# A graph attention kernel: sets of thirteen nodes in place of twelve, other first members, and the second maps and the row turn in other PSUM places

## The chip, the core and the metric

One core of one Trainium2 chip runs the whole kernel as one program. The metric is device microseconds of that core from launch to end. The kernel before took 861.07 to 866.28 us in three runs, median 863.03.

## What is computed

Eight graphs of 2048 nodes share one 0/1 matrix of neighbours. Every node has 64 features. A first attention layer with four heads and a second with one head are followed by a residual sum and a layer norm.

```python
def gat_layer(h, mask, b):                       # h: [..., N, D]
    scores = einsum('...nd,...md->...nm', h, h)
    scores = where(mask, scores, -1e16)
    return einsum('...nm,...md->...nd', softmax(scores), h) + b

B, N, C, H, D = 8, 2048, 64, 4, 64
mask = graph + eye(N) > 0
h     = einsum('bnc,hdc->bhnd', x, Wh)
out_h = gat_layer(h, mask, bh)
cat   = transpose(out_h, (0, 2, 1, 3)).reshape(B, N, H * D)
z     = leaky_relu(cat, 0.2)
h2    = einsum('bnk,dk->bnd', z, Wo)
out2  = leaky_relu(gat_layer(h2, mask, bo), 0.2)
mu, var = mean(out2, -1), mean((out2 - mu) ** 2, -1)
g     = (out2 - mu) * rsqrt(var + 1e-5) * gamma + beta
return layernorm(x + g)
```

The matrix is sparse and uneven: node n has a weight that falls with the root of n, so that the first nodes have very many neighbours and late ones few.

## The kernel before, in words

**Sets and pairs.** The first HUB = 56 nodes (the hub) attend densely to all 2048. The other 1992 make 166 sets (NS) of SET = 12 nodes each. Set s holds the nodes 56 + s + 166 k for k from 0 to 11: one of each of twelve blocks of 166 consecutive nodes. A set has one list of the nodes that any of its members has as a neighbour, at most 127 long; attention of the set is worked out against the gathered rows of that list, and a mask takes out what is not a neighbour of the member at hand. A list that doesn't fit sets a flag, and a general kernel then does all again. Two sets are a pair (NG = 83 pairs); the first layer takes one step for each pair. Four sets are a unit (NU = 42), eight sets a block (NV) in the second layer.

**First stretch.** The rows of x are loaded (`load_x` L458, the first four blocks on ACT's queue), extended and written to a table in DRAM; the hub's rows of the matrix are loaded (`hubraw` L474), and the hub's attention runs over the 16 blocks of 128 nodes (scores L621 on PE, mask L625 on DVE, exp L628 on ACT). Beside it the sets' rows of the matrix come in pieces of 10 sets by 1024 columns (`load_adj`: DMA L706, cut to 0 and 1 by POOL L711, own columns set to 1 by two selects L718). PE folds a piece to one key per column (the node's number with one bit for each member), and DVE picks the largest keys, eight at a time (`MAX` L767 and `MATCH_REPLACE` L769): these are the list. The lists are made in rounds of FIRST = 60 sets; the first round falls into the first stretch, the later ones into the loop below.

**The loop over pairs** (i from -3 to NG + 2). All engines run their own programs in the order written here; the code is scheduled by hand, and only semaphores stand between the engines. Step i holds work on several pairs:

1. scores of pair i+1 (PE L858), weighed by DVE (`weigh` L863) and exponentiated by ACT (`lift` L870)
2. head maps of pair i-1 (`project`, PE L551), leaky part on ACT (`leaky` L538), finished on DVE (L543)
3. values of pair i (`values`, PE L883), divided by their sums on DVE (`invert`: two reciprocals L890, one product L891 into `osb`)
4. a gather of the rows of pair i+5 (POOL L829), and copies on POOL
5. second maps of pair i-2 (`second_maps`, PE L917), copied out by DVE (`keep_own` L922)
6. row turn of pair i-3, a transpose (`second_rows`, PE L927); DVE adds a bias (`keep_rows` L931) and SP writes rows to a second table in DRAM
7. columns for pair i+4 (PE L843), copied out by ACT (`keep_columns` L849)
8. four transposes of gathered rows of pair i+3 (`turn`, PE L532), turned values of pair i (`turn_values`, PE L900, read by ACT in `keep_values` L907), and four more transposes

A step's picks for later lists follow on DVE behind point 6.

PSUM holds three tiles of two banks in this loop, each with one buffer: S for scores (`sp`), C for `cat`, O for `op`, and two more banks for the transposed rows. What shares a tile with what is said by columns. In `cat`, 0 to 192 of both banks hold the head maps (2 GM wide, GM = 96), 192 to 384 the columns, 384 to 480 of the first bank the second maps and 384 to 512 of the second the row turn:

```python
            ph, pr = cat[:, 0, 384:384 + GM], cat[:GM, 1, 384:512]
```

In `op`, each bank is cut in two parts of 256 columns; the first 132 of a part hold the values with their sums, and the 112 behind them the turned values:

```python
        return op.rearrange("a j (k c) -> a (j k) c", k=2)[:, :, 2 * (D + 2):2 * (D + 2) + 112]
```

In the middle of the loop, two steps for each block of eight sets, SP loads the blocks' own rows of x into `xbs` (`load_own` L961), POOL adds beta, and SP writes them to a third table (L965).

**Second layer and end.** The rows of the second table are gathered again, one list after the other (POOL L829, `rows`), with scores, exp and values on units of four sets. Every block of eight sets gets its norm (`norm`, mostly DVE), its rows of x from the third table, and is stored in eight DMAs (L1400), on SP's queue, the last block on three queues in turn.

Of the kernel before, what the change touches and what calls it, by code (L numbers as in the profile page):

```python
# [36 lines left out]
OP = mybir.AluOpType  # L37
# [7 lines left out]
HUB = 56  # L45
SET = 12
# [313 lines left out]
def fast_kernel(ctx: ExitStack, tc: tile.TileContext, x, adj, Wh, bh, Wo, bo, gamma, beta, out, flag):  # L360
# [13 lines left out]
    NS = (N - HUB) // SET  # L374
    NG = NS // 2
# [3 lines left out]
    FIRST = 60  # L379
    NR = (NS + FIRST - 1) // FIRST  # L380
    S10 = 10
    HALFN = N // 2
    NHB = (NS + S10 - 1) // S10
    assert NS * SET == N - HUB and NG * 2 == NS and HUB % 4 == 0 and NS % 2 == 0
# [31 lines left out]
    share = [const.tile([P, n], F32, name=f"share{k}") for k, n in enumerate([HALFN, HALFN, HALFN, 512, 512, 2 * 456])]  # L416
# [24 lines left out]
    es = [early.tile([P, 912], F32, name=f"e{k}") for k in range(2)]  # L441
# [31 lines left out]
    for k in range(2):  # L473
        nc.sync.dma_start(out=hubraw[k], in_=adj[0:HUB, k * NCH:(k + 1) * NCH])  # L474
# [18 lines left out]
    def make_powers():  # L493
        nc.gpsimd.memset(powers, 0.0)
        d = powers[:, :126].rearrange("p (g c) -> p g c", g=3)[:, :, :10]
        for k in range(SET):
            nc.gpsimd.affine_select(out=d, in_=d, pattern=[[0, 3], [-1, 10]], base=-10 * k, channel_multiplier=1,
                                    compare_op=OP.not_equal, fill=float(N << k))
# [6 lines left out]
        for row in (0, 32):  # L505
            nc.gpsimd.memset(adds[row:row + 1], 1.0)
        for h in range(2):
            for row, src in ((0, count[0:1, :n].unsqueeze(2).to_broadcast([1, n, SEG // 2])),
                             (32, count[32:33, h * 4:h * 4 + 4].unsqueeze(1).to_broadcast([1, n, SEG // 2]))):
                nc.vector.tensor_copy(number[row:row + 1, h, :].rearrange("p (q j) -> p q j", q=n), src)  # L510

# [71 lines left out]
    def hub_by_sets(c):  # L583
        k = slice(c * SET // 4, (c + 1) * SET // 4)
        nc.scalar.copy(hubs.rearrange("n (s k) -> n s k", k=SET)[:, :, k],
                       hubm[:, HUB:].rearrange("n (k s) -> n s k", s=NS)[:, :, k])

    def hub_mask_sets():
        pm = two("pms")
        cols = hubs  # L590
        for b in range(NHB):
            s0, ns = hub_sets(b)
            nc.tensor.matmul(pm[:ns * SET, b // 9, b % 9 * HUB:(b % 9 + 1) * HUB], cols[:, s0 * SET:(s0 + ns) * SET], identb[:HUB, :HUB],
                             start=True, stop=True)
        for b0, n in ((0, 9), (9, NHB - 10), (NHB - 1, 1)):
            np_ = hub_sets(b0)[1] * SET
            nc.vector.tensor_scalar(maskt[:np_, b0:b0 + n, :].rearrange("p b n -> p (b n)"),
                                    pm[:np_, b0 // 9, b0 % 9 * HUB:(b0 % 9 + n) * HUB], 0.0, 255.0, OP.is_equal, OP.mult)
# [54 lines left out]
    def hub_later(t, new):  # L653
# [19 lines left out]
        def to_table():  # L673
# [11 lines left out]
            dst = table2[:HUB, :].rearrange("n (q c) -> q n c", q=Q)  # L685
            for k in range(2):
                nc.sync.dma_start(out=dst[2 * t + k], in_=r[k * HUB:(k + 1) * HUB])
# [10 lines left out]
    byset = adj[HUB:, :].rearrange("(k s) m -> k s m", s=NS)  # L698

    def load_adj(r, t, m):  # L700
# [5 lines left out]
        nc.sync.dma_start(out=raw[:np_], in_=byset[:, s0:s0 + ns, m * NCH:(m + 1) * NCH])  # L706
# [6 lines left out]
        if m == 1:  # L713

            c0 = (HUB + s0) // 2
            for h in range(2):
                d = a[:np_, h, c0:c0 + NS // 2 * SET].rearrange("p (k c) -> p k c", k=SET)[:, :, :ns // 2]
                nc.gpsimd.affine_select(out=d, in_=d, pattern=[[-ns, SET], [-2, ns // 2]], base=-h,  # L718
                                        channel_multiplier=1, compare_op=OP.not_equal, fill=1.0)

    def powers_of(ns, g):
        return powers[:ns * SET, g * 32:(g + 1) * 32] if ns == S10 else powers6[:ns * SET, g, :]

    last = NS % S10
    powers6 = early.tile([120, 3, 32], BF16, name="powers6")
    if last:
        nc.gpsimd.memset(powers6, 0.0)

    def make_powers6():
        g = in_round[NR - 1] // S10 % 3  # L730
        d = powers6[:last * SET, g, 10 * g:10 * g + last]
        for k in range(SET):
# [815 lines left out]
```

## Time and profile before

| what | us |
|---|---|
| median of three runs | 863.03 |
| lowest and highest run | 861.07, 866.28 |
| the profiled execution's own time | 860.43 |
| its span (first to last instruction in the trace) | 858.6 |
| mean granted PE clock over the span | 0.97 |
| gathers of the first layer (POOL L829, 166) | 175.6 busy |
| gathers of the second layer (POOL L829, 166) | 173.7 busy |
| chain that ended last: PE, DVE, DMA | 61%, 17%, 9% of the span |

The trace is of one execution, whose own time is 1.8 us longer than its span. Busy times of an engine add up its instructions; PE is its matmuls, PEld the weight loads beside them. The chain is followed back from the last instruction to whatever released each one.

### The profile page before, as it was taken

The page shows a single profiled execution, that of the slowest core. Times are in us where ns is not written, and L with a number is a line of the kernel's source. Part 1 is how long each engine was busy: PE and PEld are TensorE (multiplying, and loading weights), DVE is VectorE, ACT ScalarE, POOL GpSimd, SP SyncE. Part 2 cuts the span into 40 slices and gives each one's busy share as a digit, 9 for nine tenths or more (in the row PEclk, how much of TensorE's full clock was granted, in tenths as well). Part 3 has the DMA queues.
Part 4 walks back from the last instruction along what each step waited for, and adds up shares of the span by engine and source line. Part 5 has one row for each costly group of instructions (what it writes and reads, how often), then busy time and mean ns, then how long its engine had stood idle before and what let it go on. Part 6 is the DMA issues. An engine that isn't in the chain of part 4 may idle for free.

```text
span 858.6 us, 42821 instructions
## 1 busy us (share of the span) xinstructions
PE 760.2 (89%) x18461; PEld 651.4 (76%) x18461; DVE 601.5 (70%) x1368; ACT 537.9 (63%) x1175; POOL 485.3 (57%) x619
## 2 busy tenths in 40 slices
PE   4798788899999999999999999998999899998940
PEld 3575567788888898988998988887887778876730
DVE  4347974688887788886556665564248999997895
ACT  2354545566666666666666666663558889887741
POOL 5444563564454456655665666504777777777700
PEclk9899989999999999999999999999999999999975
DMA  6999652443333344444444444335975666665621
GB/s 124 214 243 268 192 171 53 111 118 89 92 88 89 83 118 134 129 120 129 128 130 120 123 123 117 90 108 146 310 202 170 181 189 193 191 180 166 185 55 34
DMA packets 81791, 122.53 MB, mean 143 GB/s; under 512 B 35568, under 2 KB 51852, under 8 KB 81594
## 3 DMA queue, kind: packets, MB, share of 16 engines
q0 software_dynamic: 26784, 65.84, 28.7%
q1 hardware_dynamic: 50374, 52.71, 21.5%
q8 instruction: 148, 2.42, 1.2%
q10 hardware_dynamic: 4436, 1.15, 0.7%
q14 instruction: 49, 0.40, 0.2%
HBM read 123.91 MB, written 18.48 MB: 166 GB/s over the span
## 4 chain that ended last, share of the span: by engine, by line
PE 61%; DVE 17%; DMA 9%; issue 5%; SPq 3%; ACT 3%; POOL 2%; DVEq 0%; POOLq 0%; ACTq 0%
PE o L883 10%; PE s L858 9%; PE bank L532 8%; PE cat L843 6%; DMA rows<-table,index 5%; PE cat L551 4%; PE o L900 3%; PE cat L917 3%; PE t L532 3%; SPq L1400 3%; PE oh L639 3%; PE cat L927 2%; PE sh L621 2%; DMA out_dram<-y_s 2%; PE o L1317 2%
## 5 line engine op out<-in xcount | busy, mean ns | idle before, releaser
L829 POOL DMA_INDIRECT g<-table,index x166 | 175.6, 1058 | 173.6 <-PE o L883 144.8
L829 POOL DMA_INDIRECT rows<-table,index x166 | 173.7, 1046 | 55.1 <-issue 23.2
L863 DVE TENSOR_TENSOR e<-s,mask 128x768 f32<-128x768 f32 x83 | 79.3, 955 | 73.5 <-PE s L858 70.3
L538 ACT ACTIVATE z<-cat,bhp 128x192 f32<-128x192 f32 x166 | 60.7, 416 | 79.4 <-PE cat L551 79.3
L532 PE MATMUL t<-ident,rows 128*128 128x128 f32 x664 | 93.0, 279 | 11.2 <-DMA rows<-table,index 5.2
L883 PE MATMUL o<-g,e 128*64 128x65 f32 x2656 | 97.9, 225 | 3.9 <-issue 3.8
L532 PE MATMUL bank<-ident,g 128*128 128x128 f32 x664 | 99.5, 273 | 1.4 <-DVE e L1059 1.2
L883 PEld LDWEIGHTS o<-g,e 128*64 128x64 f32 x2656 | 85.4, 138 | 14.6 <-issue 4.8
L858 PEld LDWEIGHTS s<-y,xTg 64*64 64x64 f32 x5312 | 85.2, 135 | 13.8 <-issue 13.8
L858 PE MATMUL s<-y,xTg 64*64 64x48 f32 x5312 | 95.5, 221 | 0.0
L1436 ACT COPY xts<-t 128x512 f32<-128x512 f32 x166 | 88.7, 583 | 8.6 <-PE t L532 7.7
L532 PEld LDWEIGHTS t<-ident,rows 128*128 128x128 f32 x664 | 72.9, 141 | 24.0 <-issue 12.2
L1182 ACT COPY xTg<-bank 128x512 f32<-128x512 f32 x166 | 89.0, 596 | 2.5 <-PE bank L532 2.5
L532 PEld LDWEIGHTS bank<-ident,g 128*128 128x128 f32 x664 | 79.0, 141 | 4.1 <-issue 1.3
L849 ACT COPY y<-cat 128x384 f32<-128x384 f32 (+1 forms) x82 | 41.6, 508 | 64.1 <-PE o L900 34.5
L870 ACT ACTIVATE e<-e,shifts 128x768 f32<-128x768 f32 x83 | 80.1, 965 | 2.0 <-DVE e L863 2.0
L711 POOL TENSOR_SCALAR a<-raw 120x1024 bf16<-120x1024 int32 (+1 forms) x34 | 38.5, 1134 | 65.5 <-DMA raw<-in_adj_dram 50.6
L628 ACT ACTIVATE e<-e,shifts 128x896 f32<-128x896 f32 x32 | 33.4, 1043 | 58.1 <-DVE e L625 47.8
L890 DVE RECIPROCAL rall<-o 64x8 f32<-64x8 f32 x166 | 33.9, 205 | 47.8 <-PE o L883 46.5
L843 PE MATMUL cat<-xo,gram 128*128 128x192 f32 (+1 forms) x328 | 66.6, 326 | 0.0
L891 DVE TENSOR_TENSOR osb<-o,rall 128x512 f32<-128x512 f32 x83 | 57.4, 692 | 2.9
L625 DVE TENSOR_TENSOR e<-sh,maskh 128x896 f32<-128x896 f32 x32 | 34.8, 1087 | 31.6 <-PE sh L621 26.6
(195 smaller groups left out, 1529.8 us busy)
## 6 DMA issues: line engine op xcount, KB each, us to landing
raw<-in_adj_dram SPq DMA_DIRECT2D x32, 480.0 KB
table<-xb SPq DMA_DIRECT2D x22, 256.0 KB
xr_s<-table SPq DMA_DIRECT2D x21, 256.0 KB
table<-x SPq DMA_DIRECT2D x16, 260.0 KB
table<-rowt SPq DMA_DIRECT2D x164, 24.4 KB
xb<-in_x_dram SPq DMA_DIRECT2D x164, 24.0 KB
out_dram<-y_s SPq DMA_DIRECT2D x162, 24.0 KB
x<-in_x_dram SPq DMA_DIRECT2D x24, 128.0 KB
```

The costliest lines, as they stand in the source:

```text
L532: nc.tensor.transpose(tp[:, q * P:(q + 1) * P], rows[:, q, 1:1 + P], ident)
L538: nc.scalar.activation(z[:, hp], cat[:, :, hp * n:(hp + 1) * n], AF.Identity, bias=bhp[:, hp:hp + 1], scale=1.0)
L829: nc.gpsimd.indirect_dma_start(out=t.rearrange("n q c -> n (q c)"), out_offset=None, in_=table, in_offset=bass.IndirectOffsetOnAxis(ap=ind ...
L843: nc.tensor.matmul(cat[:, k, 2 * GM:2 * GM + n], gram[:, g % 2 * 2 + k, :], held["x", g // 2][:, :n], start=True, stop=True)
L849: nc.scalar.copy(held["y", g // 2][:, :n, g % 2 * 2:g % 2 * 2 + 2], cat[:, :, 2 * GM:2 * GM + n].rearrange("p a n -> p n a"))
L858: nc.tensor.matmul(sp[half(r), p, (q * 2 + j) * M:(q * 2 + j + 1) * M], xt[half(p), j, q, half(r)], y[half(p), (j * Q + q) * M:(j * Q + q ...
L863: nc.vector.tensor_tensor(e[:, :16 * M].rearrange("p (a q n) -> p a q n", a=2, q=Q), sp[:, :, :8 * M].rearrange("p a (q n) -> p a q n", q= ...
L870: nc.scalar.activation(e[:, :16 * M], e[:, :16 * M], AF.Exp, bias=shifts[:, 0:1], scale=1.0)
L883: nc.tensor.matmul(op[half(p), j, o0:o0 + K1], e[:, c0:c0 + 64], rw[j][:, q, sums(p)], start=True, stop=True)
L891: nc.vector.tensor_tensor(osb, v[:, :, :, 1:K1], r.unsqueeze(3).to_broadcast([P, 4, 2, D]), OP.mult)
L1182: nc.scalar.copy(t[:, k, :], bank[k])
L1436: nc.scalar.copy(xts[s // 2 % 4][:, s % 2, :], tp)
```

## The change

What it does:

- HUB becomes 60 columns of which BASE = 59 are nodes; SET becomes 13. 2048 - 59 = 1989 nodes make 153 sets. That is 77 pairs; the last pair is sets 151 and 152, so it does set 151 again (`set0`). Units are 39, the last with one set. A member's width M goes from 48 to 52, GM from 96 to 104.
- The first member of set s is no longer the node at s of the first block but the one 72 further round it (`firsts`). Nodes are thus told by positions in the order of sets, and `spans` says which runs of nodes stand at which positions. Loads of x, of the hub's rows of the matrix and stores follow these runs, in more and smaller DMAs. A piece of the matrix is 9 sets and two DMAs (108 and 9 rows); its own columns are set by six selects in place of two. A third row in `number` brings a position's key back to the node's number.
- FIRST becomes 54, 6 times 9.
- The second maps (`ph`) leave `cat` and are written into `op`, columns 132 to 236 of its first bank. The turned values go to columns 0 to 116 of each part of `op`, where the values were. The row turn (`pr`) is two transposes of 64 rows, into columns 416 to 480 of both banks of `cat`.
- The own rows of x have one buffer for two, and go in 12 DMAs for eight sets where there were 8; the stores likewise.

The diff, cut to what the prediction speaks of:

```diff
-HUB = 56
-SET = 12
+HUB = 60
+BASE = 59
+SET = 13
+ROT = 72
...
-    NS = (N - HUB) // SET
-    NG = NS // 2
+    NS = (N - BASE) // SET
+    NG = (NS + 1) // 2
...
-    FIRST = 60
+    S10 = 9
+    FIRST = 6 * S10
...
+    def firsts(s0, n):
+
+        while n > 0:
+            a = (s0 + ROT) % NS
+            w = min(n, NS - a)
+            yield s0, BASE + a, w
+            s0, n = s0 + w, n - w
+
+    def spans(p0, n):
+
+        for a, b, shift in ((0, BASE, 0), (BASE, BASE + NS - ROT, ROT), (BASE + NS - ROT, BASE + NS, ROT - NS), (BASE + NS, N, 0)):
+            lo, hi = max(a, p0), min(b, p0 + n)
+            if lo < hi:
+                yield lo, lo + shift, hi - lo
+
+    def set0(g):
+        return min(2 * g, NS - 2)
+
+    def quad(m):
+        s0 = min(4 * m, NS - 2)
+        return s0, min(4, NS - s0)
...
         for p in range(2):
-            (nc.scalar if i < 4 else nc.sync).dma_start(out=t[:, :, 1 + p * D:1 + (p + 1) * D],
-                                in_=x[p::2, i * P:(i + 1) * P, :].rearrange("q n c -> n q c"))
+            for at, node, n in spans(i * P, P):
+                (nc.scalar if i < 4 else nc.sync).dma_start(out=t[at - i * P:at - i * P + n, :, 1 + p * D:1 + (p + 1) * D],
+                                    in_=x[p::2, node:node + n, :].rearrange("q n c -> n q c"))
...
-        nc.sync.dma_start(out=raw[:np_], in_=byset[:, s0:s0 + ns, m * NCH:(m + 1) * NCH])
+        nc.sync.dma_start(out=raw[ns:np_], in_=byset[1:, s0:s0 + ns, m * NCH:(m + 1) * NCH])
+        (_, node, n), = firsts(s0, ns)
+        nc.sync.dma_start(out=raw[:ns], in_=adj[node:node + n, m * NCH:(m + 1) * NCH])
...
     OQ = 256
+    RC = 64 + M
...
     def turned(op):
-        return op.rearrange("a j (k c) -> a (j k) c", k=2)[:, :, 2 * (D + 2):2 * (D + 2) + 112]
+        return op.rearrange("a j (k c) -> a (j k) c", k=2)[:, :, :RC]
...
     def second_rows(g, pr):
-        nc.tensor.transpose(pr, held.pop(("own", g)), ident)
+        t = held.pop(("own", g))
+        for p in range(2):
+            nc.tensor.transpose(pr[:, p, :], t[half(p)], ident[half(p), half(p)])
...
-    xbs = [early.tile([P, 8, D], F32, name=f"xb{k}") for k in range(2)]
+    xbs = [early.tile([P, 8, D], F32, name="xb")]
...
         cat = one(f"cat{i}", "C") if i <= NG else None
-        if i < NG:
-            ph, pr = cat[:, 0, 384:384 + GM], cat[:GM, 1, 384:512]
-        else:
+        if i > NG:
             cat = one(f"cat{i}", "S" if i == NG + 1 else "C")
-            ph, pr = cat[:, 0, :GM], cat[:GM, 1, :P]
+        pr = cat[:GM, :, 4 * GM:4 * GM + D]
...
             op = one(f"o{i}", "O")
+            ph = op[:, 0, 2 * (D + 2):2 * (D + 2) + GM]
             values(i, op)
             invert(i, op)
+        if i >= NG:
+            ph = cat[:, 0, 2 * GM:3 * GM]
...
         if 0 <= i - 2 < NG:
             second_maps(i - 2, ph)
```

**PE, step 40 of the loop, from the last values to the turned values.** In the rows that follow the left name is what an instruction writes, the right ones what it reads (`o` is the tile `op`, `cat` the tile `cat`, `z` the leaky head maps, `own` the second maps copied out, `bank` the transposed rows, `osb` the divided values); then rows by columns, and the engines that it waits for. Before:

```order
L883 MATMUL o40_6614<-g1_81_6050,e0_110 64x65 x2
L917 MATMUL cat40_6598<-z38_6492,woT_93 64x2x4x12 [waits Activation_49]
L917 MATMUL cat40_6598<-z38_6492,woT_93 64x2x4x12 x3
L927 MATMUL cat40_6598<-ident_78,own37_6538 96x128
L843 MATMUL cat40_6598<-xo22_6406,gram_92 128x192 [waits Pool_49]
L843 MATMUL cat40_6598<-xo22_6406,gram_92 128x192
L532 MATMUL bank0_1747<-ident_78,g1_86_6398 128x128 [waits DMASW3_49,Activation_49]
L532 MATMUL bank0_1747<-ident_78,g1_86_6398 128x128 x3
L900 MATMUL o40_6614<-ident_78,osb40_6631 128x112 [waits DVE_49]
L900 MATMUL o40_6614<-ident_78,osb40_6631 128x112 x3
```

The same place of the change:

```order
L921 MATMUL o40_6886<-g1_81_6309,e0_110 64x65 x2
L955 MATMUL o40_6886<-z38_6763,woT_93 64x2x4x13 [waits DVE_49]
L955 MATMUL o40_6886<-z38_6763,woT_93 64x2x4x13 x3
L967 MATMUL cat40_6870<-ident_78,own37_6810 104x64 [waits Activation_49]
L967 MATMUL cat40_6870<-ident_78,own37_6810 104x64
L880 MATMUL cat40_6870<-xo22_6672,gram_92 128x208 [waits Pool_49]
L880 MATMUL cat40_6870<-xo22_6672,gram_92 128x208
L560 MATMUL bank0_1919<-ident_78,g1_86_6664 128x128 [waits DMASW3_49,Activation_49]
L560 MATMUL bank0_1919<-ident_78,g1_86_6664 128x128 x3
L938 MATMUL o40_6886<-ident_78,osb40_6903 128x116 [waits DVE_49]
L938 MATMUL o40_6886<-ident_78,osb40_6903 128x116 x3
```

The order of the kinds of work is the same. The second maps (L917, now L955) write `o40` where they wrote `cat40`, and wait for DVE where they waited for ACT; the row turn (L927, now L967) is two matmuls for one and now carries the wait on ACT; the turned values (L900, now L938) wait for DVE as before.

**DVE, the same step, from the reciprocals to the row copy.** `rall` holds the reciprocals of the sums, `own38` is the copy of the second maps, `rowt1` the rows for the second table. Before:

```order
L890 RECIPROCAL rall_100<-o40_6614 64x8 [waits PE_49]
L890 RECIPROCAL rall_100<-o40_6614 64x8
L891 TENSOR_TENSOR osb40_6631<-o40_6614,rall_100 128x512 [waits DVE_49]
L543 SCALAR_TENSOR_TENSOR z39_6607<-z39_6607 128x384 [waits Activation_49]
L922 COPY own38_6661<-cat40_6598 128x96 [waits PE_49,Pool_49]
L931 TENSOR_TENSOR rowt1_113<-cat40_6598,bob_95 96x128 [waits DMAHW1_49,DMAHW0_49]
```

And of the change:

```order
L928 RECIPROCAL rall_100<-o40_6886 64x8 [waits PE_49]
L928 RECIPROCAL rall_100<-o40_6886 64x8
L929 TENSOR_TENSOR osb40_6903<-o40_6886,rall_100 128x512 [waits DVE_49]
L571 SCALAR_TENSOR_TENSOR z39_6879<-z39_6879 128x416 [waits Activation_49]
L960 COPY own38_6938<-o40_6886 128x104 [waits PE_49,Pool_49]
L971 TENSOR_TENSOR rowt1_113<-cat40_6870,bob_95 104x128 [waits DMAHW4_49,DMAHW3_49,PE_49]
```

The order stands. The copy of the second maps (L960) reads `o40`, which the reciprocals and the product read too; the row copy (L971) carries a wait on PE of its own.

**ACT, at the start of the program.** `x0` and `x1` are the first two blocks of x, `whT` the transposed weights, copied out of PSUM. Before:

```order
L458 DMA x0_120<-in_x_dram 128x4x64 x2
L458 DMA x1_122<-in_x_dram 128x4x64 [waits DMAHW0_49]
L458 DMA x1_122<-in_x_dram 128x4x64 [waits DMAHW1_49]
L522 COPY whT_91<-pw_235 64x256 [waits DVE_49] x2
L614 COPY xT_102<-px0_260 128x4x128 [waits PE_49]
```

And of the change:

```order
L483 DMA x0_120<-in_x_dram 59x4x64
L483 DMA x0_120<-in_x_dram 69x4x64
L483 DMA x0_120<-in_x_dram 59x4x64
L483 DMA x0_120<-in_x_dram 69x4x64 [waits DMAHW1_49]
L483 DMA x1_122<-in_x_dram 12x4x64 [waits DMAHW5_49]
L483 DMA x1_122<-in_x_dram 72x4x64 [waits DMAHW7_49]
L483 DMA x1_122<-in_x_dram 44x4x64 [waits DMAHW0_49]
L483 DMA x1_122<-in_x_dram 12x4x64 [waits DMAHW1_49]
L483 DMA x1_122<-in_x_dram 72x4x64 [waits DMAHW2_49]
L483 DMA x1_122<-in_x_dram 44x4x64 [waits DMAHW3_49]
L550 COPY whT_91<-pw_263 64x256 [waits DVE_49] x2
```

Four loads have become ten, seven of which wait for an earlier DMA, ahead of the copy of `whT` on ACT.

More of the change, by code (lines that the diff above doesn't have):

```diff
@@ L937, in fast_kernel, with nodes @@
[L937 removed]
+            (nc.scalar if j and g >= NG - 2 else nc.sync).dma_start(out=dst[set0(g) + j], in_=r[j * Q * SET:(j + 1) * Q * SET])
+    xbs = [early.tile([P, 8, D], F32, name="xb")]
     table3 = dram.tile([NV + 1, P, 8 * D], F32, name="table3")
[L940 to L949 removed]
+    def nodes(v, ap, tile):
+        four = tile.rearrange("(t n) b d -> n t b d", n=32)
+        for a in range(2):
+            s = 8 * v + 4 * a
+            w = min(4, NS - s)
+            if w <= 0:
+                continue
+            for t in range(4):
+                p0 = t * 32 + a * SET
+                rest = ap[2 * (t % 2) + t // 2::4, BASE:, :].rearrange("f (k s) c -> k f s c", s=NS)[1:, :, s:s + w, :]
+                yield (tile[p0 + 1:p0 + SET].rearrange("p (f w) c -> p f (w c)", f=2)[:, :, :w * D],
+                       rest.rearrange("k f s c -> k f (s c)"))
+            for s1, node, n in firsts(s, w):
+                for t in range(2):
+                    k0 = s1 - s
+                    yield (four[a * SET][2 * t:2 * t + 2].rearrange("u (f w) c -> u f (w c)", f=2)[:, :, k0 * D:(k0 + n) * D],
+                           ap.rearrange("(f u v) n c -> v u f (n c)", f=2, u=2)[t, :, :, node * D:(node + n) * D])
```

174 lines of the change are left out of this document (86 added, 88 removed).

## The prediction

> **What bounds the kernel now.** First the page's head, then the busy time by stretch. I cut the span where the work changes hands: first scores of a pair of sets (132.9), last ones (572.5), first gather of the second layer (590.7), last one (813.7).
>
> ```profile
> span 858.6 us, 42821 instructions
> PE 760.2 (89%) x18461; PEld 651.4 (76%) x18461; DVE 601.5 (70%) x1368; ACT 537.9 (63%) x1175; POOL 485.3 (57%) x619
> ```
>
> ```profile
> 0.00:132.90 132.90, 103.39 (x1762) 75.61 (x1762) 77.99 (x179) 54.17 (x65) 67.16 (x139) 0.94 0.76 199
> 132.90:572.50 439.60, 423.75 (x11299) 379.80 (x11302) 307.17 (x790) 289.00 (x665) 242.13 (x308) 1.00 0.41 109
> 572.50:590.70 18.20, 15.43 (x292) 12.87 (x284) 9.28 (x24) 7.23 (x16) 1.10 (x5) 1.00 0.22 63
> 590.70:813.70 223.00, 206.45 (x4807) 174.01 (x4806) 172.47 (x314) 172.61 (x392) 172.68 (x166) 0.99 0.70 200
> 813.70:858.60 44.90, 11.17 (x332) 9.10 (x324) 34.58 (x63) 14.90 (x40) 2.21 (x3) 0.66 0.21 48
> ```
>
> Columns: length, then busy time of PE, weight loads, DVE, ACT, POOL, then clock, DMA share, GB/s. In the loop over pairs PE is busy 423.75 of 439.60 us at full clock: it is the bound there. One step of it, from the timeline:
>
> ```profile
> 344.92 1.15 PE L858 MATMUL s<-y,xTg 64*64 64x48 f32 x64
> 345.89 0.53 PE L551 MATMUL cat<-otb,whT 64*64 64x96 f32 x16
> 346.28 0.95 DVE L863 TENSOR_TENSOR e<-s,mask 128x768 f32<-128x768 f32 x1
> 346.35 1.15 PE L883 MATMUL o<-g,e 128*64 128x65 f32 x32
> 347.33 0.50 PE L917 MATMUL cat<-z,woT 128*64 128x96 f32 x8
> 347.55 0.42 DVE L890 RECIPROCAL rall<-o 64x8 f32<-64x8 f32 x2 [0.32 <-PE o L883]
> 347.76 0.32 PE L927 MATMUL cat<-ident,own 128*96 128x128 f32 x1
> 347.91 0.82 PE L843 MATMUL cat<-xo,gram 128*128 128x192 f32 x4
> 348.01 0.69 DVE L891 TENSOR_TENSOR osb<-o,rall 128x512 f32<-128x512 f32 x1
> 348.56 0.60 PE L532 MATMUL bank<-ident,g 128*128 128x128 f32 x4
> 349.00 0.55 PE L900 MATMUL o<-ident,osb 112*128 112x112 f32 x4
> 349.39 0.60 PE L532 MATMUL bank<-ident,g 128*128 128x128 f32 x4
> 349.92 1.15 PE L858 MATMUL s<-y,xTg 64*64 64x48 f32 x64
> ```
>
> The next scores start 5.00 us after the first, and every PE row starts where the row before it is issued: nothing waits. Note what lies beside: the values (L883) are issued by 347.33, DVE divides them (L890, L891) until 348.01 + 0.69 = 348.70, and PE needs the result only at 349.00. In these 1.4 us PE runs the second maps (L917), the row turn (L927), the columns (L843) and four transposes. That cover is what the change touches. 82 such intervals would be 410.0 us; the stretch has 439.6, so 29.6 us are steps held up by something else.
>
> In the second layer the gathers are the pace:
>
> ```profile
> L829 POOL DMA_INDIRECT rows<-table,index x130 | 139.2, 1071 | 39.7 <-issue 13.1 <-DMA rows<-table,index 8.9 <-PE t L532 8.2
> ```
>
> That group (window 636 to 814) is 130 gathers in 139.2 + 39.7 = 178.9 us, 1.376 each, with hardly a wait of POOL but its own 0.3 us gaps.
>
> **The change, part by part.**
>
> *Fewer pairs.* 77 instead of 83: 76 intervals instead of 82.
>
> *Longer rows in a step.* The columns go from 192 to 208 wide. A late step shows the same four matmuls at 96, with the division and the turn that follows:
>
> ```profile
> 561.54 1.15 PE L858 MATMUL s<-y,xTg 64*64 64x48 f32 x64
> 564.53 0.58 PE L843 MATMUL cat<-xo,gram 128*128 128x96 f32 x4
> 564.62 0.69 DVE L891 TENSOR_TENSOR osb<-o,rall 128x512 f32<-128x512 f32 x1
> 564.95 0.60 PE L532 MATMUL bank<-ident,g 128*128 128x128 f32 x4
> 565.38 0.58 PE L900 MATMUL o<-ident,osb 112*128 112x112 f32 x4
> 566.34 1.15 PE L858 MATMUL s<-y,xTg 64*64 64x48 f32 x64
> ```
>
> 0.65 us (347.91 to 348.56) for 192 and 0.42 (564.53 to 564.95) for 96 make 0.0024 per column, so 16 columns +0.04. Head maps and second maps from 96 to 104: by the same slope for as many passes, +0.03 each. Turned values from 112 to 116: 0.44 against 0.39 for 128 and 112 columns, so +0.01. The row turn becomes two: between 0 and one more of 0.15; I take +0.05. Scores from 48 to 52: between 0 and 0.97 × 4/48 = +0.08; 64 scores of 48 take 0.97 as 32 values of 65 take 0.98, so the width is not what limits them, and I take 0. Sum +0.16.
>
> *Second maps in the values' tile.* The order rows show L955 writing o40, the tile of this step's values, with a wait on DVE, where L917 wrote cat40 and waited on ACT. Ahead of it on DVE stand the two reciprocals and the product that read o40. So PE may start the maps only when the product is done. The late step shows the handover: product done at 564.62 + 0.69 = 565.31, L900 at 565.38, 0.07 later. In the step above PE would stand from 347.33 to 348.70 + 0.07 = 348.77: **1.44 us**. Behind L955 on PE are the row turns, columns, all transposes and the next scores, and ACT's copies wait for those; nothing moves forward into the hole, for the cover now stands behind the wait. A step becomes 5.00 + 1.44 + 0.16 = 6.60. The turn L938, which now waits for the copy L960, comes 1.8 us after the product, time enough for the rest of the leaky map and the copy.
>
> The maps write other columns than DVE reads; by addresses alone nothing would wait and a step would be 5.16. The trace of before shows such a wait between disjoint columns of one tile already:
>
> ```profile
> L917 PE MATMUL cat<-z,woT 128*64 128x96 f32 x664 | 43.5, 249 | 2.0 <-ACT z L538 1.0 <-issue 0.9
> ```
>
> L538 reads the head maps in cat, L917 writes further right in it. The Trainium skill (PSUM — Partial Sum Buffer, "PSUM bank collisions raise a hardware error") says that two engines must be kept apart by bank, not by address; by it the step is 6.60 too, the addresses alone would give 5.16.
>
> The 29.6 us of held-up steps: extra matmuls that stand between values and maps (keys of a later round, hub work) fall into the hole, DVE work that delays the copy stays. Between 0 and 29.6; I keep 10. **Loop: 76 × 6.60 + 10 = 511.6, +72.0.** Then the last step's hole and a longer end: 18.2 becomes 20.2, **+2**.
>
> *First stretch.* The hub goes from 56 to 60 columns:
>
> ```profile
> L621 PE MATMUL sh<-share,xT 64*64 64x224 f32 x512 | 35.7, 400 | 6.5 <-DVE e L625 5.7 <-DVE maskt L597 0.6
> L625 DVE TENSOR_TENSOR e<-sh,maskh 128x896 f32<-128x896 f32 x32 | 34.8, 1087 | 31.6 <-PE sh L621 26.6 <-ACT share L739 2.7 <-ACT e L628 2.2
> L628 ACT ACTIVATE e<-e,shifts 128x896 f32<-128x896 f32 x32 | 33.4, 1043 | 58.1 <-DVE e L625 47.8 <-DMA x<-in_x_dram 8.1 <-DVE x L453 2.2
> ```
>
> 4/56 of each is 2.5, 2.5 and 2.4 us. Early blocks wait for one after the other, later ones for DVE (25.80 busy of 27.00, below): between 2.5 and 7.4; I take 3.5. The loads of x0 and x1 become ten pieces instead of four on ACT, ahead of its copy:
>
> ```profile
> 14.00 0.36 ACT L522 COPY whT<-pw 64x256 f32<-64x256 f32 x1 [11.97 <-DVE gram L521]
> ...
> 29.24 1.04 ACT L628 ACTIVATE e<-e,shifts 128x896 f32<-128x896 f32 x1 [8.14 <-DMA x<-in_x_dram]
> ```
>
> ACT idles 11.97 us before the copy, which may hide all; four such pieces held it 8.14 us at 29.24. Between 0 and 8; I take 3. **+6.5** together. The adjacency pieces get a second DMA each, and six selects instead of two per 117 rows:
>
> ```profile
> L718 POOL TENSOR_SCALAR_AFFINE_SELECT a<-a 120x60 bf16<-120x60 bf16 x32 | 10.3, 345 | 1.2
> ```
>
> At most 4 × 17 × 0.345 = 23 us of POOL, which idles 65.7 of 132.9 there: 0, or up to 23 if the keys came to wait for it. The own rows' single buffer and 12 DMAs for 8 fall on SP in the middle of the loop, where no one waits for them: 0.
>
> *Second layer.* 13 gathers less: **−17.9**. The last unit has one set, so its normalisation is short; but blocks go out in 12 pieces, not 8, and SP is slow at the end:
>
> ```profile
> 843.39 11.29 SPq L1400 DMA_DIRECT2D out_dram<-y_s  x19
> ```
>
> 0.6 a piece, so four more cost 2.4, against some 6 us less of DVE work: between −6 and +4, I take **−2**.
>
> Sum, against the profiled execution's own 860.4 (span 858.6 and 1.8 around it): 860.4 + 6.5 + 72.0 + 2 − 17.9 − 2 = 921.0. The median of the runs is 863.0, 2.6 more: **923.6, say 923**.
>
> **The rivals.**
>
> *Faster: the wait replaces one.* If the product were done when PE gets to the maps, a step is 5.16: 76 × 5.16 + 29.6 = 421.8, −17.8, and with no longer end the sum is 829.2, median 832. It decides itself at 347.33: the product would have to end 1.37 us earlier. Against it: L890 waits for the values themselves, and 0.42 and 0.69 follow. Chance 0.05.
>
> *Partly hidden.* The held-up steps vanish entirely and others overlap: 875 to 898, chance 0.08.
>
> *DVE becomes late too.* The copy of rows (L971) now stands behind the columns, 1.5 us later in the step, and the picks behind it:
>
> ```profile
> 349.44 0.41 DVE L767 MAX8 share<-share 128x8 f32<-128x256 f32 x1
> ```
>
> Two picks ran from 344.44 to 346.28, 1.84 us. Counted from the scores: product 3.78, maps, turns and columns to 5.4, copy 5.7, picks 7.5; the next weighing is due at 6.60 + 1.36 = 7.96. Margin 0.4. If picks take more, each of some 50 steps loses about 0.5: 948. Chance 0.10.
>
> *PE's clock drops in the holes.*
>
> ```profile
> 73.00:77.00 4.00, 1.68 (x36) 1.21 (x38) 3.83 (x13) 1.63 (x2) 1.81 (x4) 0.98 0.94 256
> 77.00:80.40 3.40, 3.40 (x37) 2.19 (x34) 3.30 (x10) 1.04 (x1) 2.36 (x4) 0.52 0.97 282
> 81.00:108.00 27.00, 20.56 (x406) 14.07 (x400) 25.80 (x73) 14.86 (x17) 13.05 (x46) 1.00 0.71 214
> ```
>
> After 4 us with PE busy 1.68 the clock was halved for 3.4 us; over 27 us at 20.56 (76%) it stayed at 1.00. The new step has 5.16 of 6.60, 78%. At half clock it would lose 5.16 more, 76 times: about 1315. Chance 0.02. The Trainium skill (TensorE: Matmul & The Clock Gate, Part 1) halves the clock after an idle window of some 3.4 us; by it too holes of 1.44 are too short.
>
> *It doesn't do what it says:* a list of more than 127 neighbours would start the general kernel, milliseconds. In the given adjacency the longest of the 153 has 120. Under 0.01.
>
> **How the numbers follow.** The forecast has 0.75: 900 to 946 (excess 0 to 29.6, growth 0.05 to 0.3 a step, start 0 to 8). DVE late reaches to about 955. Range 898 to 952; left out are most of "partly hidden", the faster rival and the clock. A measurement tells some 0.5% from no change: faster 0.05, same 0.01, slower 0.94.
>
> **What would show it.** Right: steps of 6.6 us; idle of PE before L955, released by DVE's product L929, of about 1.44 × 76 = 109 us; the loop near 511 and at clock 1.00; 153 gathers in some 205 us. Wrong: L955 starting straight after the values; a step under 6; PE's idle put down to the copy L960 or to ACT; a first stretch more than 15 us longer.

## The result, and the profile after

The changed kernel took 940.84 us (938.17 to 942.90, four runs) and the kernel before, beside it, 864.65; the ratio is 1.0903 with a 95% interval of 1.0864 to 1.0943. Its profiled execution took 942.90 us, 1.8 more than its span. The forecast was 923, between 898 and 952.

The head of the page after:

```profile
span 941.1 us, 40516 instructions
PE 748.1 (79%) x17339; PEld 626.7 (67%) x17339; DVE 591.2 (63%) x1309; ACT 527.6 (56%) x1099; POOL 467.3 (50%) x641
```

PE does 12 us less work than before (748.1 for 760.2) in 82.5 us more. By stretch, cut at the same events (first scores, last scores, first gather of the second layer, last one), with the columns as before:

```profile
0.00:135.40 135.40, 102.46 (x1762) 73.81 (x1762) 80.52 (x181) 56.24 (x65) 69.08 (x182) 0.96 0.73 188
135.40:654.40 519.00, 425.25 (x10553) 368.77 (x10556) 307.42 (x746) 287.06 (x617) 235.12 (x301) 0.99 0.34 94
654.40:677.20 22.80, 18.50 (x277) 15.22 (x268) 9.60 (x23) 7.30 (x16) 1.11 (x5) 0.78 0.14 38
677.20:883.30 206.10, 191.42 (x4455) 160.97 (x4454) 158.58 (x287) 161.40 (x361) 159.77 (x153) 1.00 0.73 212
883.30:941.10 57.80, 10.47 (x311) 7.97 (x309) 35.09 (x73) 15.59 (x44) 2.19 (x3) 0.62 0.17 43
```

| stretch | before | after | change | forecast |
|---|---|---|---|---|
| to the first scores | 132.9 | 135.4 | +2.5 | +6.5 |
| loop over pairs | 439.6 | 519.0 | +79.4 | +72.0 |
| to the first gather of layer two | 18.2 | 22.8 | +4.6 | +2 |
| gathers | 223.0 | 206.1 | -16.9 | -17.9 |
| behind the last gather | 44.9 | 57.8 | +12.9 | -2 |

The loop is where the time went: PE is busy 425 of 519 us, where it was 424 of 440. One step of it, from the timeline (PE's rows, and DVE's product):

```profile
339.91 0.69 DVE L929 TENSOR_TENSOR osb<-o,rall 128x512 f32<-128x512 f32 x1
...
340.65 0.58 PE L955 MATMUL o<-z,woT 128*64 128x104 f32 x8 [1.25 <-DVE osb L929]
...
341.16 0.27 PE L967 MATMUL cat<-ident,own 64*104 64x64 f32 x2
...
341.36 0.97 PE L880 MATMUL cat<-xo,gram 128*128 128x208 f32 x4
...
342.17 0.60 PE L560 MATMUL bank<-ident,g 128*128 128x128 f32 x4
...
342.60 0.56 PE L938 MATMUL o<-ident,osb 116*128 116x116 f32 x4
...
343.00 0.60 PE L560 MATMUL bank<-ident,g 128*128 128x128 f32 x4
...
343.53 1.15 PE L895 MATMUL s<-y,xTg 64*64 64x52 f32 x64
...
344.50 0.55 PE L579 MATMUL cat<-otb,whT 64*64 64x104 f32 x16
...
344.99 1.15 PE L921 MATMUL o<-g,e 128*64 128x65 f32 x32
...
346.64 0.69 DVE L929 TENSOR_TENSOR osb<-o,rall 128x512 f32<-128x512 f32 x1
...
347.39 0.38 PEld L955 LDWEIGHTS o<-z,woT 128*64 128x64 f32 x8 [1.39 <-DVE osb L929]
```

From one L955 to the next are 6.74 us (340.65 to 347.39), 5.00 before. The values start at 344.99 and the maps behind them at 347.39, 2.40 later; before it was 0.98 (346.35 to 347.33). So 1.42 of the growth is the wait, released by the product, which ends at 346.64 + 0.69 = 347.33. The rest, 0.31, is spread over the other rows. The page of the profile has the wait as one group:

```profile
L955 PE MATMUL o<-z,woT 128*64 128x104 f32 x600 | 43.7, 267 | 89.2 <-DVE osb L929 89.2
```

These are 75 steps of eight matmuls, so 1.19 us each. That is less than 1.42 because the profile counts idle time only from the end that it works out for the values (344.99 + 1.15 = 346.14), and before the change the maps started 0.17 us ahead of that end.

At the end DVE is done at 850.8 before and 920.9 after, 37 us behind the last gather in both; from there to the end of the span it takes 7.8 us before and 20.2 after. Timeline of the end after:

```profile
915.86 0.35 SPq L1507 DMA_DIRECT2D flag<-fl  x1
...
920.63 0.29 DVE L1427 TENSOR_TENSOR y_s<-y_s,var_s 128x128 f32<-128x128 f32 x1 [0.60 <-ACT var_s L1418]
920.96 0.99 ACTq L1447 DMA_DIRECT2D out_dram<-y_s  x2
921.22 1.24 POOL L1447 DMA_DIRECT2D out_dram<-y_s  x2 [36.96 <-DVE y_s L1427]
924.65 12.49 SPq L1447 DMA_DIRECT2D out_dram<-y_s  x26
```

and the waits of SP's queue from 883.3 on:

```profile
SPq L1447 <- DMA out_dram<-y_s: 8.4, 1, 8.4
```

SP stood 8.4 us, though a block of twelve stores was ready, for a store that ACT could issue only when DVE had ended: in the trace ACT's store at 920.96 and the store of SP at 924.65 report to the same semaphore. Then 26 stores took 12.49 us.

The chips of the first eleven experiments took 1009 to 1018 us for the kernel before, and that of the last 863; across such chips only steps and ratios to the kernel before on the same chip are compared.

### The profile page after: what moved, and what is told of

Read it like the earlier page. It is cut to its first block, busy times and chain, and to the rows that moved or that the text cites. A ratio compares the mean times of both kernels' runs of the same rounds, so it can differ in the third digit from the quotient of the medians.

```text
span 941.1 us, 40516 instructions
## 1 busy us (share of the span) xinstructions
PE 748.1 (79%) x17339; PEld 626.7 (67%) x17339; DVE 591.2 (63%) x1309; ACT 527.6 (56%) x1099; POOL 467.3 (50%) x641
## 3 DMA queue, kind: packets, MB, share of 16 engines
q1 hardware_dynamic: 50891, 52.10, 19.5%
## 4 chain that ended last, share of the span: by engine, by line
PE 50%; DVE 21%; DMA 12%; issue 5%; SPq 4%; POOL 3%; ACT 2%; POOLq 0%; ACTq 0%; DVEq 0%
PE s L895 8%; PE o L921 8%; PE bank L560 6%; PE cat L880 6%; DVE osb L929 5%; PE o L955 4%; PE o L938 3%; DVE rall L928 3%; DMA rows<-table,index 3%; PE cat L579 3%; DMA raw<-in_adj_dram 3%; PE t L560 3%; DMA x<-in_x_dram 2%; DMA out_dram<-y_s 2%; SPq L1447 2%
## 5 line engine op out<-in xcount | busy, mean ns | idle before, releaser
L900 DVE TENSOR_TENSOR e<-s,mask 128x832 f32<-128x832 f32 x77 | 78.9, 1024 | 103.7 <-PE s L895 103.7
L566 ACT ACTIVATE z<-cat,bhp 128x208 f32<-128x208 f32 x154 | 58.4, 430 | 100.8 <-PE cat L579 100.8
L955 PE MATMUL o<-z,woT 128*64 128x104 f32 x600 | 43.7, 267 | 89.2 <-DVE osb L929 89.2
L886 ACT COPY y<-cat 128x416 f32<-128x416 f32 (+1 forms) x76 | 41.0, 540 | 121.1 <-DVE rowt L971 118.6
L955 PEld LDWEIGHTS o<-z,woT 128*64 128x64 f32 x600 | 28.5, 137 | 100.5 <-DVE osb L929 100.1
L895 PE MATMUL s<-y,xTg 64*64 64x52 f32 x4928 | 88.7, 220 | 0.0
L895 PEld LDWEIGHTS s<-y,xTg 64*64 64x64 f32 x4928 | 78.9, 134 | 12.9 <-issue 12.9
L1224 ACT COPY xTg<-bank 128x512 f32<-128x512 f32 x154 | 82.5, 596 | 2.4 <-PE bank L560 2.4
L907 ACT ACTIVATE e<-e,shifts 128x832 f32<-128x832 f32 x77 | 78.3, 1017 | 2.0 <-DVE e L900 2.0
L880 PE MATMUL cat<-xo,gram 128*128 128x208 f32 (+1 forms) x304 | 73.6, 366 | 0.0
L742 POOL TENSOR_SCALAR a<-raw 117x1024 bf16<-117x1024 int32 x34 | 38.8, 1143 | 65.6 <-DMA raw<-in_adj_dram 60.1
L657 ACT ACTIVATE e<-e,shifts 128x960 f32<-128x960 f32 x32 | 35.1, 1096 | 51.6 <-DVE e L654 46.3
```

Source lines behind the costliest of these rows:

```text
L566: nc.scalar.activation(z[:, hp], cat[:, :, hp * n:(hp + 1) * n], AF.Identity, bias=bhp[:, hp:hp + 1], scale=1.0)
L880: nc.tensor.matmul(cat[:, k, 2 * GM:2 * GM + n], gram[:, g % 2 * 2 + k, :], held["x", g // 2][:, :n], start=True, stop=True)
L895: nc.tensor.matmul(sp[half(r), p, (q * 2 + j) * M:(q * 2 + j + 1) * M], xt[half(p), j, q, half(r)], y[half(p), (j * Q + q) * M:(j * Q + q ...
L900: nc.vector.tensor_tensor(e[:, :16 * M].rearrange("p (a q n) -> p a q n", a=2, q=Q), sp[:, :, :8 * M].rearrange("p a (q n) -> p a q n", q= ...
L907: nc.scalar.activation(e[:, :16 * M], e[:, :16 * M], AF.Exp, bias=shifts[:, 0:1], scale=1.0)
L955: nc.tensor.matmul(dst, woT[:, hp, :], src, start=(hp == 0), stop=(hp == HP - 1))
```

## The experiments

**The maps behind the cover.**

```diff
-        if 0 <= i - 2 < NG:
-            second_maps(i - 2, ph)
         if 0 <= i - 3 < NG:
             second_rows(i - 3, pr)
         if 2 <= i + 4 < NG + NG % 2:
             columns(i + 4, cat)
-        if 0 <= i - 2 < NG:
-            keep_own(i - 2, ph)
         if 0 <= i - 3 < NG:
             keep_rows(i - 3, pr)
...
         if 0 <= i + 3 < NG:
             turn(bank[0], rows[1, 2 * (i + 3)])
+        if 0 <= i - 2 < NG:
+            second_maps(i - 2, ph)
+        if 0 <= i - 2 < NG:
+            keep_own(i - 2, ph)
+        if 0 <= i + 3 < NG:
+            turn(bank[1], rows[1, 2 * (i + 3) + 1])
...
         if 0 <= i < NG:
             turn_values(i, op)
             keep_values(i, op)
-        if 0 <= i + 3 < NG:
-            turn(bank[1], rows[1, 2 * (i + 3) + 1])
```

> The changed kernel with one piece moved: the second maps stand on TensorE behind the columns and the first four transposes, with their copy straight behind them on VectorE, and the second four transposes come ahead of the turned values. No instruction is added or taken out. Theory (PE stands from the last values to the end of the division, because the maps write the divided tile): the cover is back, the 1.4 us in front of the maps go to 0, a step falls from 6.73 to between 5.3 and 5.5, the whole to between 835 and 855 us. Rival (the step is long because wider matmuls cost PE more): step 6.7, whole within 5 us of 941. Second rival (the wait only moves on, to the copy of the maps that the turned values wait for): step 6.0 to 6.5, whole 885 to 925.

1025.2 us, ratio to before 1.0196 (1.0150 to 1.0241). PE's rows of a step:

```profile
287.94 1.15 PE L895 MATMUL s<-y,xTg 64*64 64x52 f32 x64
288.91 0.55 PE L579 MATMUL cat<-otb,whT 64*64 64x104 f32 x16
289.39 1.15 PE L921 MATMUL o<-g,e 128*64 128x65 f32 x32
290.47 0.27 PE L967 MATMUL cat<-ident,own 64*104 64x64 f32 x2
290.67 0.97 PE L880 MATMUL cat<-xo,gram 128*128 128x208 f32 x4
291.47 0.60 PE L560 MATMUL bank<-ident,g 128*128 128x128 f32 x4
292.00 0.58 PE L955 MATMUL o<-z,woT 128*64 128x104 f32 x8
292.51 0.66 PE L560 MATMUL bank<-ident,g 128*128 128x128 f32 x4
293.02 0.62 PE L938 MATMUL o<-ident,osb 116*128 116x116 f32 x4
```

No row of this step has a wait left. The undisturbed steps take 5.63: 1.10 less, not the 1.42 of the wait, so the step missed its range of 5.3 to 5.5. Values take 1.08 to the next row and not 0.98, the transposes ahead of the maps 0.53 and not 0.43: the new neighbours cost some 0.3. From the thirty-first step on many are longer, and the mean of all is 6.22, so the second rival holds in part: in the loop PE stands 18.6 us ahead of the turned values (L938) for the copy of the maps (L960). The loop takes 472.9 us, first to last scores. The expected 835 to 855 us can't be held against this chip; the kernel stays slower than before.

**The places alone, sets of twelve.** The kernel before with two places of the change, and then with one.

```diff
-        return op.rearrange("a j (k c) -> a (j k) c", k=2)[:, :, 2 * (D + 2):2 * (D + 2) + 112]
+        return op.rearrange("a j (k c) -> a (j k) c", k=2)[:, :, :112]
...
-            ph, pr = cat[:, 0, 384:384 + GM], cat[:GM, 1, 384:512]
+            pr = cat[:GM, 1, 384:512]
...
+            ph = op[:, 0, 2 * (D + 2):2 * (D + 2) + GM]
             values(i, op)
```

> The kernel before, sets of twelve and no rotation, with the PSUM places of the change alone: second maps in the values' tile, turned values over the values; the row turn stays. Theory: the wait comes from the place alone, so steps go from 5.00 to 6.4 and the whole from 864 to between 955 and 985 us. Rival (it takes the longer sets or the smaller rows of DMAs to make the steps long): within 10 us of 864.

1095.23 us, ratio 1.0873 (1.0792 to 1.0954). The steps are 6.47 us, 1.47 more than 5.00, near the 6.4 expected; the whole grew by 86 us, less than the 91 to 121 expected. The loop's group of second maps shows the same releaser:

```profile
L917 PE MATMUL o<-z,woT 128*64 128x96 f32 x632 | 43.9, 260 | 94.1 <-DVE osb L891 85.4 <-DVE rall L890 6.3 <-issue 2.5
```

The wait comes from the place, without the longer sets or the other loads. With only the first of these edits:

> The kernel before with only the turned values moved, to columns 0 to 112 of their tile over the values that have been divided; second maps stay where they were. Theory: no change, within 4 us of 864, since the turned values waited for the division before too. Rival (the write over the values makes PE wait): over 900 us.

1008.76 us, ratio 1.0007 (0.9973 to 1.0041): moving the turned values costs nothing. It is the second maps. Undisturbed steps of this run are 5.00 us, but on this chip the median is 5.31, so the 1.47 shows in the whole only in part.

**The changed kernel on such a chip, and other places for the maps.**

> The changed kernel as it is, to stand on the same chip as the three others of this set. Theory and rivals: steps of 6.73 us; if the gathers are as fast as in the first profile (1.35 us each in the second layer) some 941 us.

1072.02 us, ratio 1.0537 (1.0492 to 1.0582). Steps are 6.73 and the loop 517.4, as in the first profile (518.0 from first to last scores); it is the rest that takes longer. Beside it, the order untouched and the maps back in `cat`:

```diff
-            second_rows(i - 3, pr)
+            pr = one(f"pr{i}", "S")[:GM, :, :D] if i < NG else cat[:GM, :, 4 * GM:4 * GM + D]
+            second_rows(i - 3, pr)
...
+            ph = cat[:, :, 4 * GM:4 * GM + M] if i < NG else cat[:, 0, 2 * GM:3 * GM].rearrange("c (b n) -> c b n", b=2)
```

> The changed kernel with its order of work untouched and the places alone changed: the second maps go to cat, 52 columns in each bank (16 matmuls of 52 wide for 8 of 104), and the row turn into a tile of its own in the scores' place. Theory: with nothing of PE's written beside the values while DVE divides them, the 1.4 us go, a step falls from 6.73 to between 5.2 and 5.6, the loop by 85 to 115 us and the whole as much. Rival (sets of thirteen make the step long in themselves): step 6.5 or more. Second rival (the row turn or the maps now wait for another reader, ACT's leaky part or DVE's weighing): step 5.8 to 6.4.

1046.0 us, ratio 1.0280 (1.0229 to 1.0330). No L955 waits for DVE's product any more. The shortest steps take 5.36 to 5.6, as the theory has it, but the mean is 6.5, as long as the first rival has it. It isn't the sets that make it so, since the shortest steps have the same sets; it is, at least in part, a wait of the second rival's kind, for a reader that it did not name. The scores now wait for the row copy, which reads their tile and stands on DVE behind list work:

```profile
L895 PE MATMUL s<-y,xTg 64*64 64x52 f32 x4876 | 91.1, 221 | 24.7 <-DVE rowt L971 19.0 <-issue 2.6 <-DVE own L960 1.4
```

These are 19.0 us. PE stands as long again, 19.5 us, ahead of the values with no releaser in the trace, so what lengthens the steps is shown only in part. The loop fell by 22 us (517.4 to 495.5) and not by 85 to 115.

**The end.** The six stores of the last, short block were put on one queue.

```diff
-                queue = nc.sync if v < NV - 1 else (nc.sync, nc.scalar, nc.gpsimd)[k % 3]
+                queue = nc.sync if v < NV - 1 else nc.gpsimd
```

> The changed kernel with the six stores of the last, short block all on GpSimd's queue in place of three queues in turn. Theory on the 12.4 us that the end grew (from DVE's last instruction to the end of the span 20.2 us and not 7.8): SP stood 8.4 us ahead of 24 stores for the semaphore of a store that ACT could issue only when DVE had ended; without that SP starts at about 916 and the whole falls by 6 to 9 us, to 932 to 935. Rival (SP is only busy with 12 stores a block for 8): no change, within 2 us of 941.

1066.06 us, ratio 1.0576 (1.0533 to 1.0619), no gain on the 1.0537 of the changed kernel on such a chip. SP's wait for the store is gone: its last store starts 7.1 us behind DVE's end, and in the run of the changed kernel above 15.2. But the end comes 18.7 us behind DVE where it came 19.5, since SP now stands 7.0 us at the closing barrier, which fits stores of GpSimd that land late. So the wait was there, and taking it away in this manner brought nothing. With `queue = nc.sync` for all:

> The changed kernel with the six stores of the last, short block all on SP's queue in place of three in turn. Theory: SP no longer stands for ACT's store, so from DVE's last instruction to the end of the span it takes 12 to 14 us and not 20.2, and the whole falls by 6 to 8 us against the changed kernel on the same chip. Rival (as in the run with the stores on GpSimd, the end only shifts to another queue's last store): within 2 us of it.

1068.09 us to 1072.02 of the changed kernel on the same chip; the end takes 15.0 us for 19.5. The wait was worth 4.5 us at the end and 3.9 of the whole there, less than the 6 to 8 expected, for the six stores now line up behind the others. Without it the end still takes 7.2 us more than the 7.8 before. With the maps apart as well:

> Both edits together: places apart, and the last block's stores on SP. Theory: the gains add, 92 to 122 us less than the changed kernel; against the kernel before, fewer pairs and gathers (some 18 us in the second layer) stand against a step that is 0.2 to 0.6 us longer, 76 times: between 20 us faster and 10 us slower than before, 845 to 875 us where before takes 864. Rival (no gain beside the first edit): the same as places apart.

1040.37 us, ratio 1.0219 (1.0183 to 1.0256), 5.6 below places apart alone: the two add. But they are 31.7 us less than the changed kernel and not 92 to 122, for what places apart alone had missed. Before stays faster.

**The row turn.** One transpose of 128 rows in place of two of 64, in a tile of its own; the maps stay where the change has them.

```diff
-        for p in range(2):
-            nc.tensor.transpose(pr[:, p, :], t[half(p)], ident[half(p), half(p)])
+        nc.tensor.transpose(pr, t, ident)
```

> The changed kernel with the row turn as one transpose of 128 rows again, into a tile of its own in the scores' place; second maps stay in the values' tile. Reading behind it: of the 0.31 us by which a step grew beside its wait, 0.15 are the row turn itself (0.195 for 0.151) and the first of the columns behind it, which takes 0.280 to the next where the others take 0.176, since PE goes over from matmuls of 64 rows to 128. Theory: both go, a step falls from 6.73 to 6.55 to 6.62, the whole by 8 to 14 us against the changed kernel where nothing else holds the steps. Rival (the first of the columns is slow because its data come late from GpSimd or cat comes free late): only the 0.04 go, step 6.69. Second rival (scores wait for the row copy, which reads their tile now): steps that vary between 6.6 and 8.

Steps of 6.59 us for 6.73, in the range; ratio 1.0445 (1.0392 to 1.0497). The rows behind the maps:

```profile
343.75 0.32 PE L966 MATMUL pr<-ident,own 128*104 128x128 f32 x1
343.90 0.87 PE L880 MATMUL cat<-xo,gram 128*128 128x208 f32 x4
344.61 0.60 PE L560 MATMUL bank<-ident,g 128*128 128x128 f32 x4
```

Columns of 208 take 0.71 us here (343.90 to 344.61) and 0.81 behind two turns of 64 rows (341.36 to 342.17); 0.65 x 208/192 is 0.70. The columns grew as their width, and 0.10 came with the change between tile shapes ahead of them.

**All together.**

> Three edits together: second maps behind columns and transposes, row turn as one transpose into the scores' place, stores of the last block on SP. Theory: step 5.63 less 0.15, 5.45 to 5.55; on a chip where gathers and instructions come as fast as in the first profiles 845 to 860 us, 0.5 to 2% faster than before; on chips as in the two sets so far within 1% of before. Rival (sets of thirteen lose in themselves): over 1% slower than before in both.

1015.85 us, ratio 1.0036 (1.0006 to 1.0066), within the 1% expected for such a chip. The flat steps are 5.49, as expected, but from the thirty-first to the forty-fifth about every second one takes 6.7 to 6.9, and the ones between 5.8 to 6.0:

```profile
365.88 1.27 POOL L1009 TENSOR_TENSOR xb<-xb,bet 128x512 f32<-128x512 f32 x1
366.54 0.27 DVE L960 COPY own<-o 128x104 f32<-128x104 f32 x1 [1.36 <-PE o L955]
366.72 0.42 DVE L801 MAX8 share<-share 128x8 f32<-128x256 f32 x1
...
366.86 0.62 PE L938 MATMUL o<-ident,osb 116*128 116x116 f32 x4 [1.09 <-DVE own L960]
```

The copy of the maps (L960) starts 1.36 us late, and the turned values wait for it.

Giving every third store of the two blocks ahead of the last to GpSimd:

> The same, and of the two blocks ahead of the last every third store goes to GpSimd's queue. Theory: SP has 22 stores in place of 30 at the end, so from DVE's last instruction to the end it takes 10 to 12 us for 15, and the whole 3 to 5 us less than without. Rival (GpSimd's stores land late and set the end): no gain, or up to 4 us more.

1019.25 us, ratio 1.0071 (1.0041 to 1.0101): the rival holds, the end takes 17.0 us behind DVE for 14.3. At last, GpSimd's sum of beta moved behind its copy of the maps:

> The kernel with maps later, one row turn and the last stores on SP, and one piece more moved: GpSimd adds beta to a block of x (128 x 512, in every second step of the loop's second half) behind its copy of the second maps, not ahead of it. In the run without this every second step from the thirtieth on takes 6.7 us for 5.8: PE stands 1.1 us ahead of the turned values for VectorE's copy of the second maps, which doesn't start while GpSimd adds. Theory: these steps fall to 5.8 or less, the loop from 474 to between 452 and 462 us, the whole by 10 to 20 us, 0.5 to 2% faster than the kernel before on the same chip. Rival (VectorE stands for something else, the supply of its instructions for one): loop within 5 us of 474, the whole within 0.7% of before.

This run met a chip like the first: 868.29 us to 862.87 of before, ratio 1.0074 (1.0046 to 1.0102). That is not the 0.5 to 2% faster that was expected. The loop is 448.5, first to last scores, where 452 to 462 was expected, and steps thirty to forty-two take 5.49 to 5.74. Whether moving the sum did that, or the other chip, can't be told from it. The reading behind the run, that the copy doesn't start while GpSimd adds, doesn't fit the earlier trace: in the rows above the copy starts at 366.54 and the sum ends at 365.88 + 1.27 = 367.15, and the first late copy of that run, at 348.06 (1.47 us late), has no such sum beside it. What held DVE's copy stays open. By stretch:

```profile
0.00:135.80 135.80, 103.34 (x1762) 74.18 (x1762) 80.15 (x181) 56.26 (x65) 69.10 (x182) 0.96 0.71 187
135.80:585.30 449.50, 432.84 (x10453) 366.08 (x10456) 302.30 (x746) 280.11 (x617) 232.25 (x301) 0.99 0.40 109
585.30:607.70 22.40, 16.69 (x293) 13.78 (x285) 9.45 (x23) 6.84 (x15) 1.12 (x5) 0.90 0.14 38
607.70:814.00 206.30, 193.22 (x4464) 161.93 (x4460) 158.90 (x287) 162.09 (x361) 159.99 (x152) 1.00 0.74 212
814.00:866.20 52.20, 10.61 (x312) 8.11 (x310) 35.11 (x73) 15.49 (x44) 1.00 (x1) 0.64 0.18 48
```

Without the wait, with one row turn and the stores on SP, and with the sum behind, the changed kernel is 72.5 us faster (940.84 to 868.29), and the gathers keep their 17 us; but the loop is 9.9 longer than before, the end 7.3, the start 2.9 and the passage to layer two 4.2, so sets of thirteen lose by 0.7% in this form. No version was found that beats the kernel before.

## Why the prediction was right

*The hole of 1.44 us a step: right.* Measured 1.42 (2.40 less 0.98), in the 75 steps that write the maps into the divided tile, released by the product. The sign named for it, 109 us of idle time, came out at 89.2, since the hole was reckoned from where the maps started before and the profile counts from the end of the values. The two runs on places show its cause: the maps in the divided tile, and nothing else of the change. The Trainium skill (PSUM — Partial Sum Buffer, "PSUM bank collisions raise a hardware error") would have engines guarded by bank; the step of 6.73 agrees with it, and 5.16, by addresses, did not come. The maps lie in the first bank of their tile and the product reads both, so the runs don't tell a wait by bank from one by whole tile. What a program without this wait would do was not tried.

*Growth of a step, +0.16: too small, 0.31.* The slope of 0.0024 us a column, drawn through matmuls of 96 and 192 columns, was a little low: it gave 0.04 for 16 columns, and they grew by 0.05, as their width. The row turn and the columns behind it grew by 0.20 in all where 0.09 was forecast, with 0.10 of it for a change of tile shape that no term had. The second maps grew by 0.08 for 0.03 (0.51 to L967 in the step above, 0.43 before). The Trainium skill (TensorEngine Tiling (Array Packing), "Key Properties") says that a change of tiling mode drains TensorE; the 0.10 that went with the second row turn agrees, and the rule, which speaks against two turns of 64 rows, was passed over in the prediction.

*Held-up steps, 10 us: nearly right, 6.2* (the 76 intervals less 76 times their median). They do fall into the hole. Where the hole was gone they came back: 31 us in the last run, as the 29.6 before. So of the wait's 107 us (75 x 1.42) some 25 only took the place of other waits.

*Passage to the second layer, +2: 4.6. First stretch, +6.5: 2.5*, as much as the hub's four columns at one engine's pace; for the ten loads on ACT and the pieces of the matrix nothing is left. The ten loads did hold up ACT's first copy, by 6.9 us (20.91 for 14.00), but most of it fell into the wait for later blocks of x: the third exponentiation (L657, before L628) starts at 36.39 for 35.30, 1.1 later. *Gathers, -17.9: -16.9.*

*The end, -2: +12.9, the step that failed.* It had two halves. "Some 6 us less of DVE work" did not come: DVE ends 37.7 us behind the last gather for 37.1. It has four instructions of 128 x 512 less there, 0.69 us each, but twelve of 128 x 128 more for the short block, which still take 0.28 to 0.29 each. And four more stores at 0.6 were counted, but not that stores of one queue wait for another queue's, 8.4 us of SP's wait, nor that two blocks then line up behind it, 26 stores in one run. Of the 12.4 us by which the time behind DVE's end grew, the run without this wait gave back 4.5; the rest goes with more stores on one queue (30 in one run there, 19 before).

*The rivals.* "Faster" and "the clock drops" fell: L955 waits, and the loop's clock is 0.99. "DVE late" fell as well: PE stood about 1 us in all for the copy L960. "It doesn't do what it says" fell: no general kernel ran. "Partly hidden" was true as a mechanism, for the held-up steps, and priced too high.

On the profiled executions the sum was 21.9 us low (921.0 for 942.9): 14.9 of it is the end, 7.4 the loop, 3.6 the passage and the gathers, less 4.0 by which the first stretch was priced too high. That 942.9 stayed below 952 is in part luck: the end lay outside its own bounds (-6 to +4), and with held-up steps of 29.6 us, which their bounds allowed, it would have been 966.

## What to carry to other kernels

When a result moves to another PSUM tile, ask who reads that tile at that moment, and where in the writer's own queue the work stands that covered the reader: a move of place without a move of order can cost the reader's whole time in each step. Count as a cost of its own each place where TensorE goes over between tile shapes. And at a kernel's end look at which queues share completion semaphores: a store that can be issued only at the very end should not report to a semaphore for which stores of another queue, ready before it, have to wait.

## What the runs showed of the hardware that was not expected

A change between tile shapes on TensorE costs about 0.10 us: the first column matmul behind 64-row transposes is followed after 0.280 us and the others after 0.176, and transposes that follow each other every 0.11 us are followed by matmuls of 64 columns only after 0.20.

The same program takes 863 us on some chips and 1009 to 1018 on others. In the changed kernel the second layer takes 299.6 us on such a chip for 206.1. Its gathers there, from 700 to 960 us:

```profile
L866 POOL DMA_INDIRECT rows<-table,index x128 | 134.2, 1048 | 124.4 <-PE o L1362 76.6 <-issue 20.1 <-remote 13.4
```

A gather is as long as ever (1.05 us, and 1.06 on the first chip), but comes every 2.02 us ((134.2 + 124.4) / 128) and not every 1.35, since PE frees the rows later, and PE's own gaps have mostly no releaser in the trace. What makes such a chip slower stays open. The loop with its hole is as long there as on the first chip, 517.4 and 518.0, while the kernel with only the turned values moved, which takes as long as the kernel before, has a loop of 458.5 there for 438.7 of before on the first chip. This fits that the change costs 5.4% there and 9.0% here.
